# Two gated layers over four batches: how the first layer's transposed normalised x is made for batches two to four

## The chip, the core and the metric

The kernel runs on one core of a Trainium2 chip as one launch. The metric is the time of an execution on the device in microseconds (us). Engines have short names in the profile: PE is TensorE, DVE is VectorE, ACT is ScalarE, POOL is GpSimd, and SP is the engine whose queue issues the DMA transfers here. Each engine takes its instructions in the order of its own queue and waits at an instruction until what that instruction needs is there.

## The reference

The input x has 4 batches of 512 tokens with 256 values each, in float32. Two layers follow each other, and both have the same frame:

```
xn = layernorm(x)                    # over the 256 values of a token
s  = mixer(xn)                       # layer 0: xn + rmsnorm(xn @ M) * w ; layer 1: xn + causal attention
g  = silu(ffn(xn))                   # ffn: (silu(xn W1') * (xn W3')) -> Walsh-Hadamard -> W2'
x  = x + s * g
```

W1 and W3 have 1024 rows. M is a 256x256 matrix that the kernel multiplies out from layer 0's weights, and layer 1's attention normalises its input once more before it.

## The kernel before

Everything is float32. PE multiplies 12-bit parts, so each operand is kept as a pair of tiles (hi, lo) and each product is three passes: hi by hi, hi by lo, lo by hi (`mm3`). A pair is made by `split` (lines 59 to 62): ACT copies the source into hi, rounding it, and DVE subtracts hi from the source into lo. For some of layer 0's weights (`w13l`, quarters 2 and 3) POOL does the subtraction.

The work goes batch by batch: layer 0 for batches 0 to 3, then layer 1 for batches 0 to 3. The main stream of a phase is `ffn`, named f_0 to f_3 in the profile's tiles. It goes through 8 chunks of 128 hidden values. In each chunk come twelve 128x512 products into two PSUM banks (gu, from a ring of three), then silu on ACT, the product of both on DVE (tile h, line 364), a split into hh and hl, and twelve down products of 128x256 (line 332) with the W2 that went through the Walsh-Hadamard transform. The up products need xn transposed, with the 256 values on the partitions: the pair xth, xtl of [128, 2, 512].

Beside a phase's main stream run other tasks, cut into steps by `yield`. `Beside` hands them out evenly over the 16 slots of a phase, from the counts `NORM, MIXER, ATT, ATT1, W2P = 3, 3, 18, 6, 12` (line 570). In layer 0 they are:

- `gate` of the batch before: x += s * silu(down result), on ACT and DVE.
- `mixer(b)`: products with M on PE (tile o), copies and squares on ACT, a pow on POOL (ssr, line 420), four scalings on DVE (osb, line 422) and one addition xn + osb of 128x1024 on POOL (line 425).
- `norm(0, b + 1)`: the next batch's normalisation, which the change is about.
- In phase 0 also the preparation of layer 0's weights (`prep_first`), in phase 1 the preparation of layer 1's W2 (`prep_w2`: butterflies w2b on DVE, lines 125 and 126, a split into w2bh and w2bl, products on PE, splits from PSUM into w2h and w2l), and in phase 2 the first normalisation of layer 1.

The order written in the code is not the order in the queues: the framework's scheduler orders each engine's instructions when the program is built. Tiles come from pools. `t4` has ten slots of 512 KB for raw weights, osb, mrb and others, so a load into such a slot waits until the slot's last reader is done.

Before the change, `norm(0, b)` for b = 1 to 3 takes the moments of each token on DVE, the pow on POOL (`ln_r`), and four DVE operations that make xn token by token. Then for each half k of the 256 values `transpose_half` lets PE transpose four 128x128 tiles into a PSUM bank (tile xt_2tp and its like, line 248), and `split` reads this bank. Batch 0 has its own way, `norm_first`. `norm(1, b)` in layer 1 ends with another chain: the second moments (tile mr) are transposed on PE from [128, 8] to [8, 128] (tile mrp), copied by ACT (rows), written by a DMA to DRAM (there) and read back by a second DMA into all 128 partitions (mrb, 512 KB).

Of the kernel before, what the change touches and what calls it, by code (L numbers as in the profile page):

```python
# [11 lines left out]
F32 = mybir.dt.float32  # L12
# float32 kept to the 12 significant bits that one pass of the tensor engine multiplies
# exactly. A float32 value is the exact sum of two of these (hi + lo), so a float32 product
# is three passes: hi*hi + hi*lo + lo*hi; lo*lo lies below float32's rounding.
F32R = mybir.dt.float32r
# [19 lines left out]
def kernel(ctx: ExitStack, tc: tile.TileContext, a: dict, out: bass.AP):  # L36
# [7 lines left out]
    def t4(name, shape, dt=F32):  # L44
        return act.tile(shape, dt, tag="t4", name=name, bufs=10)
# [13 lines left out]
    def split(src, hi, lo, engine=nc.vector):  # L59
        """hi + lo = src, exactly."""  # L60
        nc.scalar.copy(hi, src)  # L61
        engine.tensor_tensor(lo, src, hi.bitcast(F32), ALU.subtract)

    def mm3(o, terms):
        """o = sum over terms of lhs.T @ rhs, each operand a pair (hi, lo)."""
        seq = [(l[0], r[0]) for l, r in terms]
        for l, r in terms:
            seq += [(l[0], r[1]), (l[1], r[0])]
        for n, (l, r) in enumerate(seq):
            nc.tensor.matmul(o, l, r, start=n == 0, stop=n == len(seq) - 1)  # L70

# [1 line left out]
    xs = {}  # L73

# [3 lines left out]
    def load_x(b, nt=NT):  # L78
        xs[b] = x_slot(f"x{b}", [P, NT, D])
        src = a["x"][b].rearrange("(t p) d -> p t d", p=P)  # L80
        for t in range(0, NT, nt):
            nc.sync.dma_start(xs[b][:, t : t + nt, :], src[:, t : t + nt, :])

    ident, had_f, mask = (wp.tile([P, P], F32, name=n) for n in ("ident", "had_f", "mask"))
# [28 lines left out]
    def prep_w2(layer, raws, dst, scratch):  # L113
        """Rows of W2 under the Walsh-Hadamard transform (it is symmetric, so it may act on
        W2 in place of the hidden values): over the 8 blocks by butterflies, over the 128
        rows of a block by a product with the +-1/32 matrix."""
        w2h, w2l = dst
        for half in range(2):
            ds_ = slice(half * P, (half + 1) * P)
            cur = raws[half]  # L120
            for st, h in enumerate((1, 2, 4)):
# [6 lines left out]
                yield  # L128
            # in float32 it costs TensorE two passes more, but no split beforehand
            native = layer == 0 and half == 0  # L130
# [22 lines left out]
    def product_of_weights(name, lhsT, rhs, nk, scale=None):  # L153
        """[256, 256] = lhsT.T @ rhs over nk chunks of 128, in float32, as a (hi, lo) pair."""
        hi = wp.tile([P, 2, D], F32R, name=f"{name}h")
# [22 lines left out]
    def prep_m(win, wout):  # L178
        """xi*(sum of C_real*B_real - C_imag*B_imag) between W_in and W_out is one matrix."""
        cb = wp.tile([P, 4, 2, DS], F32, name="cb")  # L180
# [29 lines left out]

# [1 line left out]
    def moments(name, x, mr):  # L212
        """mr[:, 0] = the tokens' means, mr[:, 1] = their 1 / sqrt(variance + eps)"""
        st = act.tile([P, NT, 6], F32, tag="stats", name=f"{name}st", bufs=4)
# [9 lines left out]
    def layernorm(name, x, y, groups=(NT,)):  # L224
        """y = layernorm(x), the token tiles in groups of these sizes"""
        t0 = 0
# [36 lines left out]
    def norm_first():  # L263
        """norm(0, 0), each token tile on its own"""
        xn = act.tile([P, NT, D], F32, tag="xn", name="xn0_0", bufs=3)
# [4 lines left out]
        for t in range(NT):  # L270
# [3 lines left out]
            split(o, hi[:, :, sl(t)], lo[:, :, sl(t)])  # L274

    def norm(layer, b):
        xn = act.tile([P, NT, D], F32, tag="xn", name=f"xn{layer}_{b}", bufs=3)
        hi = act.tile([P, 2, S], F32R, tag="xt", name=f"xth{layer}_{b}", bufs=4)
        lo = act.tile([P, 2, S], F32R, tag="xt", name=f"xtl{layer}_{b}", bufs=4)
        xns[layer, b], xTs[layer, b] = xn, (hi, lo)  # L280
        layernorm(f"ln{layer}_{b}", xs[b], xn)
        yield
        if layer:
            # The second normalisation acts on the transposed values: its moments as rows of
            # all tokens, in every partition.
            mr = act.tile([P, 2, NT], F32, tag="mr", name=f"mr{b}", bufs=2)
            moments(f"ln2_{b}", xn, mr)
            yield
            o = psum(f"mrp{b}", [2 * NT, P])
            nc.tensor.transpose(o, mr.rearrange("p a t -> p (a t)"), ident)  # L290
            rows = act.tile([2 * NT, P], F32, tag="rows", name=f"rows{b}", bufs=1)
            nc.scalar.copy(rows, o)
            there = dram.tile([2 * NT, P], F32, tag="rows", name=f"there{b}")
            nc.sync.dma_start(there, rows)
            mrb = t4(f"mrb{b}", [P, 2, S])
            nc.sync.dma_start(
                mrb, there.rearrange("(a t) p -> a (t p)", a=2).unsqueeze(0).to_broadcast([P, 2, S])
            )
            mrs[b] = mrb
            yield  # L300
            return
        for k in range(2):
            o = transpose_half(f"xt{layer}_{b}", xn, k)
            split(o, hi[:, k, :], lo[:, k, :])
            yield

# [3 lines left out]
    def ffn(name, xT, w13, w2, slot, defer=1, spare=(), last=None, parts=1, behind=False):  # L310
        """Up, silu gate, down with the transformed W2: two PSUM banks of two token tiles.
        The down products of a chunk follow the up products of the defer-th after it.
        spare: pairs of tiles that hold the split hidden values of the first chunks.
        last: called with each token tile's result, finished one after the other, each in a
        bank of its own."""
        w2h, w2l = w2
# [7 lines left out]
        def down(c, hh, hl, tiles=range(NT)):  # L324
            for t in tiles:
                o = outs[t]
                for n, (l, r) in enumerate(((hh, w2h), (hh, w2l), (hl, w2h))):
# [7 lines left out]

                    # A start clears the accumulate bits of its whole bank: the bank's second
                    # tile begins without one, behind the first's.
                    if first and t % 2 == 1 and last is None:
# [39 lines left out]
        if last is None:  # L378
            for q in queue:
                down(*q)  # L380
            return dn
        # the later tokens' products stay behind, for the ends of the earlier tokens to run beside
        (q0, q1, q2, q3), ts_ = queue, range(NT)
# [10 lines left out]
    def gate(name, dn, s, x, store=None):  # L394
        """x += s * silu(dn), a pair of token tiles at a time."""
        for i in range(2):
# [8 lines left out]
    def mixer(b):  # L405
        """xn += rmsnorm(xn @ M) * norm_w"""
        xn, xT, m = xns[0, b], xTs[0, b], first["m"]
# [20 lines left out]
    def attention(b):  # L428
        """The transposed xn, split; then xn += causal attention of the normalised, scaled and
        shifted xn"""  # L430
        xn, wqk, wvo = xns[1, b], first["wqk"], first["wvo"]
# [29 lines left out]
        def scores(i0):  # L461
            """Masked scores of two query tiles"""
            if i0:
# [10 lines left out]
        def softmax(i0, scs):  # L474
            """The two exponentials follow each other, for ScalarE changes its table for them."""
            nmax = act.tile([P, 2], F32, tag="nmax", name=f"nmax{b}_{i0}", bufs=4)
# [53 lines left out]
    class Beside:  # L530
        """Steps of other work, spread over the slots of a feed-forward block."""

# [26 lines left out]
    def some(gen, n):  # L559
        """The next n steps of gen"""  # L560
        for _ in range(n):
            next(gen)
            yield
# [4 lines left out]

    # steps of each; an attention's first ones (up to its scores) run a phase ahead of the rest
    NORM, MIXER, ATT, ATT1, W2P = 3, 3, 18, 6, 12  # L570

# [1 line left out]
    load_x(0, 1)  # L573
    # TensorE's clock rises only after a while of work: these products of zeros run while the
    # first loads are under way.
    zeros = hid("zeros")
# [44 lines left out]

# [1 line left out]
    dn = None  # L623
# [35 lines left out]

# [1 line left out]
    def store(b):  # L661
# [38 lines left out]
def _rows(w):  # L700
    """[r*128, n] -> [128, r, n]"""
    return w.reshape(-1, P, w.shape[1]).transpose(1, 0, 2)


def _w13(w1, w3):
    """Columns of W1.T and W3.T in turns of 128, in four parts of [128, 2, 512]."""
    w = np.stack([w1.T.reshape(2, P, NH, P), w3.T.reshape(2, P, NH, P)], axis=3)
    return w.reshape(2, P, 4, S).transpose(2, 1, 0, 3)


def _w2(w2):
    """W2.T as [half of d][128, 8 blocks, 128]."""
    return w2.T.reshape(NH, P, 2, P).transpose(2, 1, 0, 3)
# [45 lines left out]
```

## Time and profile before

| | |
|---|---|
| median of 3 runs | 374.34 us (374.17 to 375.75) |
| profiled execution, first to last instruction | 370.9 us |
| the profiled execution's own whole time | not listed apart; the runs' median lies 3.4 us above its span |
| PE busy | 361.5 us (97%), 2167 instructions |
| DVE busy | 248.0 us (67%), 519 instructions |
| ACT busy | 179.7 us (48%) |
| POOL busy | 36.2 us (10%), 30 instructions |
| one broadcast mrb<-there, 512 KB, from issue to landing | 3.7 us |
| one load x<-in_x, 512 KB, from issue to landing | 3.7 us |

The profile is of one execution. A line of a timeline has the start in us, the duration in us, the engine, the source line, the operation, and "out<-in" by the tiles' names; "x2" means that two instructions are drawn together in it, and the bracket at the end is idle time before it and the instruction that ended it. Matmuls are pipelined and overlap each other in these lines, so PE's pace is read from one start to the next. The slices cut the span in 40 equal parts, a digit being the busy share in tenths. A wait counts only where an engine on the chain of waits has to sit through it.

### The profile page before, as it was taken

The numbers are of one execution on the slowest core, as the hardware profiler recorded it, in microseconds if no ns is written. First come the engines' busy times: TensorE is split into PE (matmuls) and PEld (weight loads), VectorE is DVE, ScalarE is ACT, GpSimd is POOL, SyncE is SP. The second block draws the span as 40 slices with busy tenths as digits, with TensorE's granted clock in tenths as the row PEclk, the third lists the DMA queues.
The fourth block names the chain that finished last, engine by engine and source line by source line (L and its number), as shares of the span: only waits on it lengthen the run. The fifth ranks groups of instructions, "written<-read, shape, count | busy, mean of one in ns | idle before, by whom it ended". The sixth has DMA issues, their size and how long they took to land.

```text
span 370.9 us, 5491 instructions
## 1 busy us (share of the span) xinstructions
PE 361.5 (97%) x2167; PEld 318.2 (86%) x2167; DVE 248.0 (67%) x519; ACT 179.7 (48%) x334; POOL 36.2 (10%) x30
## 2 busy tenths in 40 slices
PE   6997999999999999999999999999999999999995
PEld 4875999888888898889888998988989898888895
DVE  6898948996499339945949487465846447374644
ACT  2765334624453335445553654266633646356451
POOL 2060023410025002400011000010000000000000
PEclk9999999999999999999999999999999999999999
DMA  7915200000000040110010001100003000010001
GB/s 234 389 51 203 80 2 1 2 0 2 0 3 0 0 171 0 58 57 2 1 59 0 0 2 57 59 1 2 0 2 114 2 0 1 2 57 2 1 2 57
DMA packets 8969, 15.50 MB, mean 42 GB/s; under 512 B 848, under 2 KB 6640, under 8 KB 8944
## 3 DMA queue, kind: packets, MB, share of 16 engines
q1 hardware_dynamic: 8944, 15.16, 11.7%
q8 instruction: 17, 0.28, 0.3%
q14 instruction: 8, 0.07, 0.1%
HBM read 13.04 MB, written 2.11 MB: 41 GB/s over the span
## 4 chain that ended last, share of the span: by engine, by line
PE 90%; DVE 5%; DMA 2%; SPq 1%; issue 0%; ACT 0%; DVEq 0%
PE f_3gu L70 12%; PE f_2gu L70 12%; PE f_1gu L70 12%; PE f_0gu L70 8%; PE f_0dn L332 6%; PE f_3dn L332 6%; PE f_1dn L332 6%; PE f_2dn L332 6%; PE sc L70 4%; PE pv L70 4%; PE o L70 3%; PE v L70 3%; PE tq L70 3%; DMA w2raw<-in_w 2%; DVE w2b L125 1%; PE pt L498 1%
## 5 line engine op out<-in xcount | busy, mean ns | idle before, releaser
L70 PE MATMUL f_0gu<-xtl,w13h 128*128 128x512 f32 (+1 forms) x68 | 25.8, 382 | 0.0
L70 PE MATMUL f_1gu<-xth,w13l 128*128 128x512 f32 x64 | 25.5, 399 | 0.0
L70 PE MATMUL f_0gu<-xth,w13l 128*128 128x512 f32 (+1 forms) x68 | 25.5, 384 | 0.0
L70 PE MATMUL f_3gu<-xtl,w13h 128*128 128x512 f32 x64 | 25.5, 398 | 0.0
L70 PE MATMUL f_2gu<-xth,w13l 128*128 128x512 f32 x64 | 25.3, 396 | 0.0
L70 PE MATMUL f_3gu<-xth,w13l 128*128 128x512 f32 x64 | 25.3, 396 | 0.0
L70 PE MATMUL f_1gu<-xtl,w13h 128*128 128x512 f32 x64 | 25.3, 396 | 0.0
L70 PE MATMUL f_2gu<-xtl,w13h 128*128 128x512 f32 x64 | 25.3, 395 | 0.0
L70 PE MATMUL f_0gu<-xth,w13h 128*128 128x512 f32 (+1 forms) x68 | 21.3, 393 | 2.5 <-DVE f_0h L364 2.5
L364 DVE TENSOR_TENSOR f_2h<-f_2h,f_2gu 128x512 f32<-128x512 f32 x16 | 10.9, 681 | 19.1 <-PE f_2gu L70 11.0
L61 ACT CAST f_2hh<-f_2h 128x512 fp32r<-128x512 f32 x16 | 9.9, 621 | 23.0 <-DVE f_2h L364 23.0
L70 PE MATMUL f_2gu<-xth,w13h 128*128 128x512 f32 x64 | 20.7, 397 | 0.0
L70 PE MATMUL f_1gu<-xth,w13h 128*128 128x512 f32 x64 | 20.7, 398 | 0.0
L70 PE MATMUL f_3gu<-xth,w13h 128*128 128x512 f32 x64 | 20.6, 397 | 0.0
L61 ACT CAST f_3hh<-f_3h 128x512 fp32r<-128x512 f32 x16 | 9.9, 620 | 19.7 <-DVE f_3h L364 19.7
L332 PE MATMUL f_3dn<-w2l,f_3hh 128*128 128x256 f32 x64 | 17.6, 281 | 0.0
L332 PE MATMUL f_2dn<-w2l,f_2hh 128*128 128x256 f32 x64 | 17.6, 282 | 0.0
L332 PE MATMUL f_3dn<-w2h,f_3hh 128*128 128x256 f32 x64 | 17.5, 281 | 0.0
L332 PE MATMUL f_2dn<-w2h,f_2hh 128*128 128x256 f32 x64 | 17.5, 281 | 0.0
L332 PE MATMUL f_1dn<-w2l,f_1hh 128*128 128x256 f32 x64 | 17.4, 281 | 0.0
L332 PE MATMUL f_1dn<-w2h,f_1hh 128*128 128x256 f32 x64 | 17.3, 281 | 0.0
L363 ACT ACTIVATE f_2h<-f_2gu 128x512 f32<-128x512 f32 x16 | 9.5, 596 | 16.0 <-PE f_2gu L70 16.0
(227 smaller groups left out, 1104.4 us busy)
## 6 DMA issues: line engine op xcount, KB each, us to landing
w13raw<-in_w SPq DMA_DIRECT2D x8, 512.0 KB, 6.2
w2raw<-in_w SPq DMA_DIRECT2D x4, 512.0 KB, 6.8
mrb<-there SPq DMA_DIRECT2D x4, 512.0 KB, 3.7
x<-in_x SPq DMA_DIRECT2D x3, 512.0 KB, 3.7
out<-x SPq DMA_DIRECT2D x6, 256.0 KB, 2.1
x<-in_x SPq DMA_DIRECT2D x4, 128.0 KB, 2.2
qkraw<-in_qk SPq DMA_DIRECT2D x1, 512.0 KB, 4.7
voraw<-in_vo SPq DMA_DIRECT2D x1, 512.0 KB
```

Source lines behind the costliest of these rows:

```text
L61: nc.scalar.copy(hi, src)
L70: nc.tensor.matmul(o, l, r, start=n == 0, stop=n == len(seq) - 1)
L125: nc.vector.tensor_tensor(nv[:, :, 0], cv[:, :, 0], cv[:, :, 1], ALU.add)
L332: return nc.tensor.matmul(o, l[:, sl(t)], r[:, c, :], start=start, stop=stop, skip_group_check=True)
L363: nc.scalar.activation(h, gu[0], AF.Silu)
L364: gates.append(nc.vector.tensor_tensor(h, h, gu[1], ALU.mult))
L498: nc.tensor.transpose(pt[:, sl(j)], p[:, sl(j)], ident)
```

## The change

For batches 1 to 3 of layer 0, PE no longer transposes the normalised x. The host hands over a transposed copy of the input (`xT`), of which 512 KB a batch are loaded into a tile xTraw. `norm_both` takes the tokens' mean and 1/sqrt(variance + eps) (tile mr), sends them through the chain mrp, rows, there, mrb that layer 1 already had (now a function, `rows_everywhere`), makes xn token by token as before for the mixer and the gate, and then normalises the transposed copy on DVE: for each half, a subtraction of the broadcast means, a multiplication by the broadcast factors, and the split, whose source is now in SBUF. The step count of a normalisation goes from 3 to 4. Layer 1 does the same as before. Comments were dropped, which is left out here.

```diff
     def load_x(b, nt=NT):
...
+        if b:
+            xTraw[b] = t4(f"xTraw{b}", [P, 2, S])
+            nc.sync.dma_start(xTraw[b], a["xT"][b])
...
+    def rows_everywhere(name, mr):
+        o = psum(f"mrp{name}", [2 * NT, P])
+        nc.tensor.transpose(o, mr.rearrange("p a t -> p (a t)"), ident)
+        rows = act.tile([2 * NT, P], F32, tag="rows", name=f"rows{name}", bufs=1)
+        nc.scalar.copy(rows, o)
+        there = dram.tile([2 * NT, P], F32, tag="rows", name=f"there{name}")
+        nc.sync.dma_start(there, rows)
+        mrb = t4(f"mrb{name}", [P, 2, S])
+        nc.sync.dma_start(
+            mrb, there.rearrange("(a t) p -> a (t p)", a=2).unsqueeze(0).to_broadcast([P, 2, S])
+        )
+        return mrb
+
+    def norm_both(b):
...
+        mr = act.tile([P, 2, NT], F32, tag="mr", name=f"mr0_{b}", bufs=2)
+        moments(f"ln0_{b}", x, mr)
+        yield
+        mrb = rows_everywhere(f"0_{b}", mr)
+        for t in range(NT):
+            nc.vector.tensor_scalar(
+                xn[:, t, :], x[:, t, :], mr[:, 0, t : t + 1], mr[:, 1, t : t + 1],
+                ALU.subtract, ALU.mult,
+            )
+        yield
+        for k in range(2):
+            f = xTraw[b][:, k, :]
+            nc.vector.tensor_tensor(f, f, mrb[:, 0, :], ALU.subtract)
+            nc.vector.tensor_tensor(f, f, mrb[:, 1, :], ALU.mult)
+            split(f, hi[:, k, :], lo[:, k, :])
+            yield
+
     def norm(layer, b):
+        if layer == 0:
+            yield from norm_both(b)
+            return
...
-        for k in range(2):
-            o = transpose_half(f"xt{layer}_{b}", xn, k)
-            split(o, hi[:, k, :], lo[:, k, :])
-            yield
...
-    NORM, MIXER, ATT, ATT1, W2P = 3, 3, 18, 6, 12
+    NORM, MIXER, ATT, ATT1, W2P = 4, 3, 18, 6, 12
...
         "x": v["L0_attn_x"],
+        "xT": v["L0_attn_x"].transpose(0, 2, 1).reshape(B, 2, P, S).transpose(0, 2, 1, 3),
```

More of the change, by code (lines that the diff above doesn't have):

```diff
@@ L70, in mm3 @@
             nc.tensor.matmul(o, l, r, start=n == 0, stop=n == len(seq) - 1)
-    xs = {}
+    xs, xTraw = {}, {}
     def x_slot(name, shape):
@@ L274, in norm_first @@
             split(o, hi[:, :, sl(t)], lo[:, :, sl(t)])
+    def rows_everywhere(name, mr):
[11 more added lines that the diff above has]
+    def norm_both(b):
+        xn = act.tile([P, NT, D], F32, tag="xn", name=f"xn0_{b}", bufs=3)
+        hi = act.tile([P, 2, S], F32R, tag="xt", name=f"xth0_{b}", bufs=4)
+        lo = act.tile([P, 2, S], F32R, tag="xt", name=f"xtl0_{b}", bufs=4)
+        xns[0, b], xTs[0, b] = xn, (hi, lo)
+        x = xs[b]
+        mr = act.tile([P, 2, NT], F32, tag="mr", name=f"mr0_{b}", bufs=2)
[14 more added lines that the diff above has]
+            yield
     def norm(layer, b):
+        if layer == 0:
+            yield from norm_both(b)
+            return
         xn = act.tile([P, NT, D], F32, tag="xn", name=f"xn{layer}_{b}", bufs=3)
@@ L282, in norm @@
         yield
-        if layer:
-            mr = act.tile([P, 2, NT], F32, tag="mr", name=f"mr{b}", bufs=2)
-            moments(f"ln2_{b}", xn, mr)
-            yield
[L289 to L301, printed above, removed]
-        for k in range(2):
-            o = transpose_half(f"xt{layer}_{b}", xn, k)
-            split(o, hi[:, k, :], lo[:, k, :])
-            yield
+        mr = act.tile([P, 2, NT], F32, tag="mr", name=f"mr{b}", bufs=2)
+        moments(f"ln2_{b}", xn, mr)
+        yield
+        mrs[b] = rows_everywhere(str(b), mr)
+        yield
     def after(ins):
```

## The prediction

> **What bounds the kernel now.** I read the page's slices and chain first, then the tables by stretch, then the order in time of PE, VectorE (DVE) and GpSimd (POOL) around the lines that the diff touches.
>
> ```profile
> PE   6997999999999999999999999999999999999995
> PEclk9999999999999999999999999999999999999999
> PE 90%; DVE 5%; DMA 2%; SPq 1%; issue 0%; ACT 0%; DVEq 0%
> ```
>
> PE is full in every slice behind the fourth, at a full granted clock, and holds 90% of the chain. From one PE start to the next (0.233 us behind a 128x512 product, 0.118 behind a 128x256 one) no gap is left from 42 us to the end. So PE work taken out there shortens the run one for one, and a wait put in there lengthens it one for one. Other engines count where PE waits for them. The last such wait lies in the start stage, and the chain shows what the removed work is:
>
> ```profile
> 31.43 0.73 PE L70 MATMUL f_0gu<-xth,w13h 128*128 128x512 f32 x2 [2.50 <-DVE f_0h L364]
> ```
> ```profile
> 70.82 0.87 PE xt_2tp L248 x8
> ```
>
> How near DVE is to being the bound, by stretch (columns: length, then busy time of PE, weight loads, DVE, ACT, POOL):
>
> ```profile
> 0.00:36.00 36.00, 30.55 (x133) 23.34 (x134) 30.39 (x56) 18.55 (x31) 8.74 (x11) 1.00 0.62 213
> 58.00:95.00 37.00, 37.00 (x215) 32.32 (x214) 29.99 (x55) 16.13 (x33) 6.11 (x4) 1.00 0.01 1
> 95.00:133.00 38.00, 38.00 (x229) 33.37 (x229) 25.63 (x58) 15.63 (x33) 6.85 (x5) 1.00 0.05 20
> ```
>
> The second row is batch 1's phase: DVE is busy 30 of 37 us there, for it carries the preparation of layer 1's W2 beside the rest. PE doesn't wait, but narrowly: chunk 2's low half f_1hl ends at 79.48 and its down product starts at 79.94 (0.46 us of slack), chunk 3's f_1h ends 80.08 for 80.89 (0.8).
>
> Why DVE is late at times, though its operations are short, stands in the lines of DVE and POOL together:
>
> ```profile
> 20.31 6.31 POOL L62 TENSOR_TENSOR w13l<-w13raw,w13h 128x1024 fp32r<-128x1024 f32 x2 [13.46 <-ACT w13h L61]
> 55.69 2.41 POOL L425 TENSOR_TENSOR xn<-xn,osb 128x1024 f32<-128x1024 f32 x1 [1.85 <-DVE osb L422]
> 73.00 2.41 POOL L425 TENSOR_TENSOR xn<-xn,osb 128x1024 f32<-128x1024 f32 x1 [1.85 <-DVE osb L422]
> ```
> ```profile
> 21.45 0.68 DVE L364 TENSOR_TENSOR f_0h<-f_0h,f_0gu 128x512 f32<-128x512 f32 x1
> 22.04 2.32 DVE L62 TENSOR_TENSOR early<-f_0h,early 128x512 fp32r<-128x512 f32 x1
> 24.29 2.88 DVE L125 TENSOR_TENSOR w2b<-w2b 128x512 f32<-128x512 f32 x1
> ```
> ```profile
> 73.36 3.12 DVE L62 TENSOR_TENSOR w2bl<-w2b,w2bh 128x1024 fp32r<-128x1024 f32 x1
> ```
> ```profile
> 56.00 1.29 DVE L62 TENSOR_TENSOR xtl<-xt_1tp,xth 128x512 fp32r<-128x512 f32 x2 [0.45 <-ACT xth L61]
> ```
>
> A DVE operation with two SBUF inputs (early, w2b, w2bl) takes 2.3 to 3.1 us while a POOL operation runs, against 0.68 or 1.23 alone; one that reads PSUM (f_0gu, xt_1tp) is not delayed. The splits that the change removes are of the second kind, and all that it puts in their place are of the first.
>
> **The change, part by part.** The sum is made on the profiled execution's span, 370.9 us; the median of the runs, 374.34, lies 3.4 above it, for what is around the span, and I add that at the end.
>
> *PE.* Out go 8 transposes a batch, 0.87 us in the row above, 24 in all: -2.6. In comes one transpose of 8 rows a batch (mrp), about 0.11 each: +0.3. Net -0.77 a batch, -2.3 in all, all of it on the bound engine.
>
> *DVE's own work.* Per batch, four 128x512 operations come in (two subtractions, two multiplications) at a step of 0.60 us (17.84 to 18.44 to 19.04 among its rows): +2.4. moments() in place of layernorm() adds a copy of 128x4, below 0.2. The two splits stay, from SBUF now. [...] I take 0.
>
> *The new chain.* Moments, pow on POOL (1.0), mrp on PE, rows on ACT, two DMAs on SP, then DVE. Layer 1 has the same chain: rows at 127.98 for 0.25, its DMA at 128.26, the broadcast issued 1.28 later, landing 3.7 later (page). So 5.2 us from mrp's end to the values in all partitions. Before, PE itself handed x over.
>
> *DMAs.* Six 512 KB transfers more (three xTraw, three mrb) and three small ones, all on SP; ACT and POOL issue none. x1 to x3 and xTraw1 are issued by 37 us. Behind them SP waits in order for rows0_1 (50.5), and w2raw of layer 1, before at 33.8, is issued behind it, at about 53. Landing takes 5.3 to 8.4 by its own rows: 58 to 61, with its first use at 62.85. I take 0; at worst 1 us more of crowding on DVE. xTraw3's slot and the other transfers have tens of us. POOL's order changes too: three pows (1.0 each) stand ahead of the first mixer's; their moments are ready by 47 to 50, so 0.
>
> *Start stage.* The scheduler's order for DVE changes: the next W2 butterflies (w2b<-w2b, two SBUF inputs) now stand ahead of f_0h's multiplication of chunk 2, which before ran at 21.45 untouched by POOL. They get caught under the w13l operations, and f_0h behind them ends near 27.3 in place of 22.1. PE then waits from 24.6 to about 27.4, and 0.65 more for w2bh; the 2.5 to 2.7 us wait at 31.43 falls away in exchange. Net +0.75, bounds -0.5 (the butterflies get in before POOL) and +2 (both waits stay in part).
>
> *Batch 0 to 1.* PE would reach f_1's first product at 57.9 (58.0 less 0.78 of transposes, plus 0.75 of lag). mrp0_1 stands behind the mixer's products, at about 49; rows 50.3, its DMA 50.6, broadcast 51.9, landed 55.6. But POOL's addition xn0+osb runs from about 54.9 to 57.3, and the subtraction has two SBUF inputs. So: start 57.25, subtraction, multiplication and half the second pair to 59.05, ACT's cast (0.55) to 59.6, PE at 59.7. Wait: +1.8. Without the lock 0.5; with the DMAs at their upper durations 2.5. [...]
>
> *Batch 1.* The same four operations for batch 2 (2.4 us) enter the stretch in which DVE has 7 us free of 37 and PE's slack is 0.46 to 0.8, with DVE 1.7 behind at its start. In my walk of DVE's new order with the old durations chunk 2's f_1h ends at 77.9, w2bl (again under POOL's addition) at 81, and f_1hl at 84. PE waits 0.8, 1.2, 1.1 and 0.2 for these: +3.3, bounds +1 (order kinder, DVE catches up in its idle spots) and +4.5.
>
> *Batch 2.* DVE waits in its queue for mrb0_3 (about 1.9 us; mrp0_3 sits late in the phase), and f_2's hidden values queue behind it. Their slack here is 1.0 at the least and mostly over 2: 0, bounds 0 and +1. Later phases have slacks of 2 us and more and unchanged work: 0.
>
> Sum: -2.3 + 0.75 + 1.8 + 3.3 = +3.55, span 374.5, time 377.9. As a wait in the start stage lets DVE catch up a little for the next, I shade it to 377.5.
>
> **Rivals.** A, as above, chance 0.55: 375.9 to 380.5. B, chance 0.21: the same mechanism, but one of the two large waits is absorbed (by the slack at the boundary, xth's 2.05 us in the trace of before, or by DVE's 7 idle us): +0.3 to +1.7, so 374.6 to 376.0. C, the other side, chance 0.14: DVE never gets behind PE. Its place is the w2bl under POOL's addition at 73; if the shifted phases take these two apart, each of the waits of batch 1 (3.3) and the port's part of the boundary (1.3) falls off and what is left is PE's 2.3 against 0.75 and 0.5: about -1.0, and with no wait at all -2.3 (-2.8 with the start's lower bound): 371.5 to 373.3, the lower half likelier, for what spares batch 1 spares the boundary too. It decides where the new DVE work delays chunk 2's and 3's values by less than their 0.46 to 0.8 us. Against it: 2.4 us of new work in front of a 0.46 us slack. D, chance 0.10: the delays feed back through the ring of three PSUM banks of the up products, PE's waits delay DVE's inputs and so on: +7 (5 to 9), so 381. That the change doesn't take the transposes off PE is excluded by the code: xt of layer 0 is gone for batches 1 to 3.
>
> **How the numbers follow.** The likeliest case gives 377.5. About 0.5% (1.9 us, so 372.5 to 376.2) is what a measurement of this kernel can tell from no change. A lies above it for nearly all of its width (0.53 of 0.55), D wholly (0.09 counted); B lies within, with the rest of A and D; C counts 0.12 below and 0.02 within. Faster 0.12, same 0.26, slower 0.62. The range leaves out D's upper half and C's tail: 372.0 to 381.5.
>
> **What would show it.** Right: between 57 and 60 us a PE wait of 1 to 2.5 us, on ACT's xth with DVE's subtraction at 2 us or more beside POOL's addition; PE waits of some 3 us in 75 to 90, on f_1h and f_1hl, with a w2bl of 3 us near; a PE wait at about 25 in place of the one at 31; busy PE about 2.3 less; no PE wait in batch 2. Wrong: no PE gap behind 45 us (then about 372), or a gap for w2raw, xTraw or mrb3, which I priced at nothing.

## The result, and the profile after

The changed kernel takes 376.23 us (median of 14 runs, 375.21 to 377.82), the kernel before 373.78 in the same comparison (median of 14). The ratio is 1.007, with a 95% interval of 1.0051 to 1.0089: slower by 1.9 to 3.3 us. The profiled execution after has a span of 375.8 us and took 377.55 as a whole, 1.3 above its median; what lies around a span is thus 1.75 us. Single executions lie up to 3.7 us apart before and 2.6 after, so below waits are compared by the traces and times by medians and ratios.

The page of the changed kernel, in the same lines as shown of before:

```profile
PE   7979998989999999999999999999999999999995
PEclk9998999999999999999999999999999999999999
PE 87%; DVE 6%; DMA 2%; POOL 2%; ACT 1%; issue 1%; SPq 0%; DVEq 0%; POOLq 0%
```

A slice is 9.4 us here. PE's row has an 8 at 56 and at 75 us, where before it was full, and the chain holds a POOL share of 2%. From 85 us on the row is as before. The 8 in the clock's row, at 28 us, is told of in the last section. In the table by stretch (length, then busy time of PE, weight loads, DVE, ACT, POOL, then granted clock), batch 1's phase stands out:

```profile
36.00:58.00 22.00, 22.00 (x149) 20.39 (x148) 15.48 (x54) 8.87 (x23) 5.82 (x5) 1.00 0.22 62
58.00:95.00 37.00, 33.64 (x192) 28.57 (x192) 34.81 (x61) 16.62 (x35) 6.79 (x3) 1.00 0.17 61
95.00:133.00 38.00, 38.00 (x224) 33.15 (x223) 23.95 (x57) 15.85 (x34) 5.91 (x4) 1.00 0.10 32
```

DVE went from 30.0 to 34.8 busy us of 37, PE lost 3.4. Batch 2's phase, behind it, has no PE wait. The timeline of PE names every wait, in the brackets:

```profile
26.78 0.73 PE L70 MATMUL f_0gu<-xth,w13h 128*128 128x512 f32 x2 [2.20 <-DVE f_0h L391]
...
61.05 0.74 PE L70 MATMUL f_1gu<-xth,w13h 128*128 128x512 f32 x2 [1.04 <-ACT xth L61]
...
79.38 0.73 PE L70 MATMUL f_1gu<-xth,w13h 128*128 128x512 f32 x2 [0.61 <-DVE f_1h L391]
...
82.34 0.74 PE L146 MATMUL w2ps<-w2bl,had 128*128 128x512 f32 x2 [0.82 <-DVE w2bl L62]
...
85.35 0.39 PE L359 MATMUL f_1dn<-w2h,f_1hl 128*128 128x256 f32 x1 [0.88 <-DVE f_1hl L62]
```

Measured from one start to the next, less the step of the product in front, these waits are 2.4 (start stage), 1.20 (into batch 1), and 0.78, 0.99 and 1.04 in batch 1; one of 0.15 follows at 90.5. I use this measure from here on. Behind 42 us they add up to 4.16. Less the 2.3 us of PE work saved, that is +1.85; with +0.6 from the start stage (first experiment) the sum is +2.45, the measured difference of the medians. That they agree to the last digit is luck, for the interval of the ratio is 1.4 us wide.

Why DVE was late in batch 1 is in the timelines of POOL and of DVE, first after the change, then before it:

```profile
56.19 2.40 POOL L452 TENSOR_TENSOR xn<-xn,osb 128x1024 f32<-128x1024 f32 x1 [1.79 <-DVE osb L449]
73.22 3.80 POOL L447 TENSOR_TENSOR ssr<-ssr,mhalf 128x4 f32<-128x4 f32 x1 [14.63 <-DVE ssr L446]
78.80 2.40 POOL L452 TENSOR_TENSOR xn<-xn,osb 128x1024 f32<-128x1024 f32 x1 [1.79 <-DVE osb L449]
```
```profile
57.90 1.84 DVE L312 TENSOR_TENSOR xTraw<-xTraw,mrb 128x512 f32<-128x512 f32 x2 [1.79 <-DMA mrb<-there]
...
77.05 1.67 DVE L449 SCALAR_TENSOR_TENSOR osb<-osb,ssr,nwb 128x256 f32<-128x256 f32 x4 [0.91 <-POOL ssr L447]
78.64 0.68 DVE L391 TENSOR_TENSOR f_1h<-f_1h,f_1gu 128x512 f32<-128x512 f32 x1
79.24 3.05 DVE L62 TENSOR_TENSOR w2bl<-w2b,w2bh 128x1024 fp32r<-128x1024 f32 x1
```
```profile
68.56 2.59 POOL L420 TENSOR_TENSOR ssr<-ssr,mhalf 128x4 f32<-128x4 f32 x1 [3.27 <-DVE ssr L419]
```
```profile
71.18 1.67 DVE L422 SCALAR_TENSOR_TENSOR osb<-osb,ssr,nwb 128x256 f32<-128x256 f32 x4 [0.90 <-POOL ssr L420]
72.77 0.68 DVE L364 TENSOR_TENSOR f_1h<-f_1h,f_1gu 128x512 f32<-128x512 f32 x1
```

The pow on four values a partition takes 1.01 us in most places and 3.80 here in the changed kernel: between 73.05 and 76.14 DVE runs two-input operations back to back (w2b, the new multiplications on xTraw, f_1hl), each at 0.68 to 0.69, and this time POOL's operation is the one drawn out. DVE then waits 0.91 at osb for the pow, f_1h stands behind osb in its queue, and PE waits 0.78 for f_1h. POOL's addition falls on w2bl, which takes 3.05 in place of about 1.23, and PE waits 0.99 for w2bl and 1.04 for f_1hl, which stands behind it. Where the prediction and the expectations speak of a lock or of a shared port, these lengths are what is measured; what in the chip draws the operations out, no run shows.

Neither collision is new. Before the change the pow took 2.59, DVE waited 0.90 for it at osb, and w2bl took 3.12 under the addition (the prediction shows that line). PE had slack for it: f_1h of chunk 2 ended at 73.44, 2.5 us before the product that needs its bank started at 75.97. After the change this f_1h ends at 79.32, 5.9 us later, while PE's queue gets there only 2.6 later. Of the 3.3 between them, 2.4 are the four new operations; the rest DVE brings along from its late entry into the phase (its first operation of the gate starts 4.0 later than before, PE's first product 3.0).

### The profile page after: what moved, and what is told of

The parts are those of the page before. It is cut to its first block, busy times and chain, and to the rows that moved or that the text cites. A ratio compares the mean times of both kernels' runs of the same rounds, so it can differ in the third digit from the quotient of the medians.

```text
span 375.8 us, 5490 instructions
## 1 busy us (share of the span) xinstructions
PE 363.9 (97%) x2146; PEld 318.3 (85%) x2146; DVE 254.1 (68%) x534; ACT 180.5 (48%) x337; POOL 36.4 (10%) x30
## 4 chain that ended last, share of the span: by engine, by line
PE 87%; DVE 6%; DMA 2%; POOL 2%; ACT 1%; issue 1%; SPq 0%; DVEq 0%; POOLq 0%
PE f_3gu L70 12%; PE f_2gu L70 12%; PE f_0gu L70 10%; PE f_1gu L70 10%; PE f_3dn L359 6%; PE f_2dn L359 6%; PE f_1dn L359 5%; PE sc L70 4%; PE pv L70 4%; PE f_0dn L359 4%; PE o L70 3%; PE v L70 3%; PE tq L70 3%; DVE w2b L128 1%; DVE w2b L129 1%; DMA mrb<-there 1%
## 5 line engine op out<-in xcount | busy, mean ns | idle before, releaser
L70 PE MATMUL f_0gu<-xth,w13h 128*128 128x512 f32 (+1 forms) x68 | 22.2, 406 | 2.2 <-DVE f_0h L391 2.2
L61 ACT CAST f_1hh<-f_1h 128x512 fp32r<-128x512 f32 x16 | 9.9, 620 | 15.7 <-DVE f_1h L391 15.7
```

## The experiments

Each ran against the kernel before. "Over" is the ratio less one, times that kernel's median of 373.3 to 373.5 us.

**1. The start stage by itself.** The diff changes one number that looks like bookkeeping: a normalisation counts as 4 steps, and `Beside` hands out steps by that count. Here the kernel before has the new count in phase 0 and nothing else.

```diff
-            tasks.append((norm(0, b + 1), NORM))
+            tasks.append((norm(0, b + 1), NORM if b else 4))
```

> The kernel before with one number changed: the step count of the normalisation in phase 0 is given as 4 instead of 3 (the steps themselves stay 3). It moves the W2 butterflies of the start ahead of f_0h as in the changed kernel; nothing else of the change is in it. Theory (the start stage's order costs by itself): the PE wait near 31 us goes, one near 24 to 27 comes, +0.3 to +1.0 us over before. Rival (the two waits swap for nothing, the whole loss lies behind 57 us): within 0.2 us of before.

Measured: 375.02 against 373.46, ratio 1.0029 (1.0005 to 1.0053). DVE's order in the start is that of the changed kernel, and the wait moved from 28.5 to 24.2 with a second one behind it:

```profile
27.04 0.73 PE L70 MATMUL f_0gu<-xth,w13h 128*128 128x512 f32 x2 [2.43 <-DVE f_0h L364]
...
30.58 0.74 PE L142 MATMUL w2ps<-w2bh,had 128*128 128x512 f32 x2 [0.48 <-ACT w2bh L61]
```

Summed from start to start, less the median step of each form of product, PE loses 10.96 us in this trace and 10.35 in before: +0.6. The ratio says +1.1. The difference is in line with the clock that is listed with each run: runs with a mean of 0.993 to 0.995 take about 2 us longer in this comparison than those near 1.0 (last section), and 8 of the 12 runs here are such, but 10 of before's 29. Run against run at the higher clock the medians differ by 0.5 (373.15 and 372.65), at the lower one by 0.6 (375.19 and 374.61). So the start stage's cost is real, and it comes from a step count, not from the new operations.

**2. The changed kernel with that count put back** to 3 in phase 0.

> The changed kernel with the step count of the normalisation in phase 0 put back to 3, so that the start stage has the order of before. Theory: the changed kernel's time less what the start stage costs, 0.3 to 1.0 us, so +1.4 to +2.1 us over before, with the waits at 60 us and in 78 to 91 us as they were. Rival (start order free): +2.4 us as the changed kernel.

Measured: 378.35, ratio 1.0132 (1.01 to 1.0164), +4.9 us; a clear miss. The wait into batch 1 is 3.23 us here, not 1.20:

```profile
60.40 0.82 PE L70 MATMUL f_1gu<-xth,w13h 128*128 128x512 f32 x2 [3.07 <-ACT xth L61]
```

The count had also moved mrp0_1 in PE's queue. Call the PE work that is queued between mrp0_1 and f_1's first product the cover. Counted in the queue and priced at 0.233 and 0.118 us a product, it is 8.85 us in the changed kernel and 6.84 here. The chain from mrp to xth is equally long in both: mrp at 50.8 and the product at 61.05, and 50.2 and 60.40. So the wait is about 10.1 less the cover: 1.2 and 3.2. Behind the long wait PE's 128x512 products lie 0.43 us apart until 64.2 instead of 0.233 (granted clock 0.95 over 58 to 95 us), which took about 1.6 more. The listed clock of all six runs is 0.990 to 0.995.

**3. Only batches 2 and 3 the new way.** Batch 1 keeps PE's transposes (`if layer == 0 and b in (2, 3)`), and the start stage is that of before.

> Only batches 2 and 3 are normalised the new way, batch 1 by PE as before: no change of the start stage and no late hand-off between batch 0 and 1, but the four additional VectorE operations for batch 2 lie in batch 1's phase. Theory (crowding of VectorE in batch 1's phase under POOL's lock makes the waits by itself): 1.5 us of PE work saved, waits of 1.5 to 3 us there, so 0 to +1.5 us over before. Rival (those waits come only because VectorE enters the phase late): no waits, -1.5 us.

Measured: 375.66, ratio 1.0056 (1.0033 to 1.0078), +2.1 us. The waits in batch 1's phase are 1.12, 0.75, 0.92, 0.43 and 0.24, together 3.5, more than I gave them. Less 1.5 of PE work that is +1.9. DVE enters the phase on time here, so the late entry isn't needed for these waits. The collision is another one: the pow takes 1.02 and w2bl 1.21, but POOL's addition (3.92 in place of 2.40) meets a pair of the new multiplications, which takes 2.89 in place of 1.29:

```profile
76.73 3.92 POOL L457 TENSOR_TENSOR xn<-xn,osb 128x1024 f32<-128x1024 f32 x1 [4.46 <-DVE osb L454]
```
```profile
78.91 2.89 DVE L313 TENSOR_TENSOR xTraw<-xTraw,mrb 128x512 f32<-128x512 f32 x2
```

**4. No POOL addition in batch 1's mixer.**

```diff
-        nc.gpsimd.tensor_tensor(xn, xn, osb, ALU.add)
+        if b != 1:
+            nc.gpsimd.tensor_tensor(xn, xn, osb, ALU.add)
```

> The changed kernel without POOL's addition xn+osb of batch 1 (so batch 1's s lacks the mixer's product; the output differs for that batch). Theory (the shared port makes w2bl late): w2bl takes 1.2 instead of 3.05 us, and the PE waits at 81 and 84 us (1.0 each) go while the first of 0.8 at 78.5 stays: 2 us below the changed kernel, +0.4 us over before. Rival (VectorE has simply too much to do there): w2bl shorter, but the waits stay within 0.4 us, +2.0 to +2.4 us over before.

Measured: 374.46, ratio 1.003 (1.001 to 1.0051), +1.1 us where I expected +0.4, and 1.8 us below the changed kernel's median. In its DVE timeline w2bl is back to its own length:

```profile
78.31 1.22 DVE L62 TENSOR_TENSOR w2bl<-w2b,w2bh 128x1024 fp32r<-128x1024 f32 x1
```

Of the three waits the first stays (0.77), the second is gone, and the third is 0.31. The pow still takes 3.80.

**5. Neither POOL instruction in batch 1's mixer:** the pow of ssr is left out too (`if b != 1:` ahead of it). DVE's work is the changed kernel's.

> The changed kernel without POOL's two instructions in batch 1's mixer: neither the pow of ssr nor the addition xn+osb (batch 1's s is wrong for it). VectorE's work is as in the changed kernel. Theory (the waits of batch 1 are the shared port's: the first because POOL's pow is locked out for 3.8 us by VectorE's back-to-back operations and osb and f_1h stand behind it in VectorE's queue, the second and third because the addition locks out w2bl): all three waits go, none over 0.3 us is left in 62 to 95 us, 2.5 to 3 us below the changed kernel, -0.5 to 0 us against before. Rival (too much VectorE work for the phase): waits of 0.8 us or more stay.

Measured: 373.37 against 373.39, ratio 1.0 (0.9977 to 1.0023). Two waits of 0.12 and 0.16 are left in batch 1's phase, and w2bl and f_1h are on time, with DVE as full as in the changed kernel:

```profile
58.00:95.00 37.00, 36.00 (x206) 30.95 (x207) 33.43 (x63) 18.72 (x38) 0.00 (x0) 1.00 0.11 36
```

(The 1.0 us that PE misses here is the wait into batch 1, unchanged at 1.20, whose greater part lies behind 58.) DVE's fullness alone makes PE wait for almost nothing. That the first wait is due to the pow being drawn out to 3.80, and not to there being a pow, wasn't run apart; but an undisturbed pow (1.01 from 73.22) would be done before DVE comes to osb at 76.14.

**6. Without the four new operations for batch 2:** its transposed x goes unnormalised into the split, and POOL's two instructions stay.

```diff
-            nc.vector.tensor_tensor(f, f, mrb[:, 0, :], ALU.subtract)
-            nc.vector.tensor_tensor(f, f, mrb[:, 1, :], ALU.mult)
+            if b != 2:
+                nc.vector.tensor_tensor(f, f, mrb[:, 0, :], ALU.subtract)
+                nc.vector.tensor_tensor(f, f, mrb[:, 1, :], ALU.mult)
```

> The changed kernel without the subtractions and multiplications of batch 2 (its transposed x is used as loaded, so batch 2's result is wrong): 2.4 us of two-input VectorE work less in batch 1's phase, with POOL's pow and addition kept and w2bl still behind osb and f_1h in VectorE's queue. Theory (the new operations are what pushes POOL's two and VectorE's later ones together): the waits of 3.0 us in 78 to 91 us shrink to 0 to 0.8, so 2.2 to 3 us below the changed kernel. Rival (the port's collisions come by the order alone, whoever fills VectorE): 1.5 us or more of them stay.

Measured: 373.96, ratio 1.0011 (0.9988 to 1.0034), 2.3 below the changed kernel; no wait in batch 1's phase. w2bl is still caught under POOL's addition, while the pow takes 1.01:

```profile
76.65 2.83 DVE L62 TENSOR_TENSOR w2bl<-w2b,w2bh 128x1024 fp32r<-128x1024 f32 x1
```

So it takes both. The collisions with POOL cost DVE 0.9 and 1.8 us, which PE's slack covered before; 2.4 us of new operations use that slack up. The ratio shows less than the trace, by which this version would be 0.5 below before (-2.3 + 0.6 + 1.2): 10 of its 12 runs are at the lower clock, and 7 of before's 35.

**7. Only batch 1 the new way.**

> Only batch 1 is normalised the new way. Theory (parts add up): start stage +0.6, boundary wait +1.2 or a little more as PE comes to it earlier, 0.8 saved, no wait in batch 1's phase beyond: +1.0 to +1.5 us over before. Rival (batch 1's waits come from the late entry into the phase, not from batch 2's new operations): the 3 us of waits come as well, +3.5 to +4.5 us.

Measured: 374.38, ratio 1.0034 (1.0014 to 1.0055), +1.3 us. There is a wait of 1.03 into batch 1 (cover counted as above 9.09, so the chain is 10.1 again) and none in its phase. The parts add up: 0.6 + 1.0 - 0.8 = +0.8, within the interval (0.5 to 2.1).

**8. Only batch 3 the new way.**

> Only batch 3 is normalised the new way. Theory (batch 2's phase has slack enough for the late broadcast and the additional VectorE work): PE does 0.77 us less and waits for nothing new, -0.8 us against before. Rival (the late mrb0_3 or f_2's hidden values cost something there): 0 or above.

Measured: 373.09 against 373.26, ratio 0.999 (0.9976 to 1.0005). PE has no new wait behind 42 us. The 0.8 us saving lies within the interval, but the runs don't tell it from nothing.

**9. The normalisation ahead of the mixer in phase 0.** If the wait into batch 1 is chain less cover, the chain has to start earlier in PE's queue.

```diff
+        if b == 0:
+            tasks.append((norm(0, 1), NORM))
         tasks.append((mixer(b), MIXER))
-        if b + 1 < B:
-            if b:
-                load_x(b + 1)
+        if b and b + 1 < B:
+            load_x(b + 1)
             tasks.append((norm(0, b + 1), NORM))
```

> The changed kernel with batch 1's normalisation ahead of batch 0's mixer in the list of tasks of phase 0, so that mrp0_1 has 12.2 us of PE work (by the steps 0.233 and 0.118) between itself and f_1's first product instead of 8.9. Theory (the wait at the boundary is the length of the chain mrp to xth, 10.2 us, less that cover): the wait of 1.2 us goes, 1.2 us below the changed kernel, +1.0 to +1.4 us over before, with the waits in 78 to 91 us kept. Rival (the port and VectorE's queue set it): the wait stays at 0.8 us or more.

Measured: 372.54 against 373.26, ratio 0.9971 (0.9954 to 0.9989): faster than before. The wait into batch 1 is gone, ACT's xth being complete at 55.9 for PE at 58.2, as forecast; but the waits within batch 1 are gone too, which I had not forecast. In the timelines of POOL and DVE both collisions are gone:

```profile
67.62 1.02 POOL L447 TENSOR_TENSOR ssr<-ssr,mhalf 128x4 f32<-128x4 f32 x1 [6.62 <-DVE ssr L446]
70.43 2.79 POOL L452 TENSOR_TENSOR xn<-xn,osb 128x1024 f32<-128x1024 f32 x1 [1.78 <-DVE osb L449]
```
```profile
82.71 1.22 DVE L62 TENSOR_TENSOR w2bl<-w2b,w2bh 128x1024 fp32r<-128x1024 f32 x1
```
```profile
58.00:95.00 37.00, 37.00 (x214) 32.23 (x213) 33.11 (x61) 17.26 (x35) 6.20 (x3) 1.00 0.08 30
```

The second fence is DVE's line of w2bl, the third the row of batch 1's phase. The mixer's part of DVE's and POOL's work comes earlier in the phase, so the pow meets no run of two-input operations (1.02), and w2bl comes 9 us after the addition instead of under it. Whether that or the earlier place of the mixer's work counts for more was not tested. DVE is as full as ever (33.1 of 37), and PE is full.

**10. As 9, with the step count of phase 0 at 3.**

```diff
-            tasks.append((norm(0, 1), NORM))
+            tasks.append((norm(0, 1), 3))
```

> The changed kernel with the normalisation ahead of the mixer in phase 0 and the step count of phase 0 at 3 (the start stage in the order of before); layer 1's W2 stays in phase 1. Theory (both repairs add): the start stage's 0.6 us comes off the version with the normalisation ahead, no wait behind 45 us, -1.3 to -2.0 us against before, 0.4 to 0.9 us below the version with the normalisation ahead alone. Rival (the other order brings the port's collisions in batch 1 back): waits of 1 us or more in 62 to 95 us, at or above before's time.

Measured: 372.05 against 373.39, ratio 0.9962 (0.9942 to 0.9981), -1.4 us, the fastest version. No PE wait lies behind 42 us. Two short ones at 37 and 38 us (0.6 and 0.24) are new, waits for w2h and for f_0h in the start stage, and keep it from the full 2.3. It is not told from version 9 by these intervals.

```profile
PE 361.1 (98%) x2146; PEld 316.5 (86%) x2146; DVE 252.4 (68%) x534; ACT 180.8 (49%) x337; POOL 37.1 (10%) x30
```

**11. As 10, and layer 1's W2 prepared in phases 1 and 2** (5 and 7 of its 12 steps, `some(w2_steps, 5)` in phase 1 and the rest in phase 2), to empty batch 1's phase.

> The changed kernel with three orders altered: the normalisation ahead of the mixer in phase 0, the step count of phase 0 at 3 as in before, and the preparation of layer 1's W2 spread over phases 1 and 2 (5 and 7 of its 12 steps) instead of all in phase 1. Theory (each PE wait of the changed kernel comes from where the work was put, not from the new work itself): no new PE wait, only the saving of 2.3 us on PE, -1.5 to -2.3 us against before. Rival (VectorE's four operations a batch are too many wherever they lie): waits come up in phase 2, -0.5 to +1.5 us.

Measured: 372.08, ratio 0.9974 (0.9952 to 0.9997), about -1.0 us. It is faster than before, but the rival's waits do come up in phase 2: 0.49 at 115 us and 0.52 at 121. It gains nothing over version 10, which needs no split.

**12. The same split in the kernel before,** as a control.

> Control: the kernel before with the preparation of layer 1's W2 spread over phases 1 and 2 in the same way. PE waits for nothing there in before, so both theories expect no difference, within 0.3 us.

Measured: 373.45, ratio 1.0013 (0.9999 to 1.0027). The time agrees with no difference, my premise doesn't: PE waits 0.22 and 0.75 us at 117 to 118 us, for w2bh and for f_2's hl. Phase 2 had less room than its 25.6 busy us of 38 suggested.

## Why the prediction was right, and where it was off

The result lies in the forecast range, on the forecast side, by the mechanism of case A, at the lower end of A's 375.9 to 380.5. The signs of all terms were right, and their sum was too high. By its terms:

- *PE's saving, -2.3.* Shown by the count (2167 to 2146 instructions: 24 out, 3 in) and by experiments 9 and 10, where nearly only it is left: with the small waits of their start stages it adds up to -1.2 and -1.5, and the ratios give -1.1 and -1.4. The sign that I named for it, "busy PE about 2.3 less", was a bad one: busy PE rose from 361.5 to 363.9, since a matmul's record was longer at half rate (0.63 us for a 128x512 product at 28.16 us, 0.39 at 27.35), and in front of a wait a product counts with its whole record (0.40 at 24.19) instead of its step (0.233). Starts and counts tell PE's work, its busy sum doesn't.
- *Start stage, +0.75.* 0.6 by the trace of experiment 1. Its cause is the step count.
- *Batch 0 to 1, +1.8.* 1.20. I made POOL's addition the deciding share, 1.3 of it (1.8 less the 0.5 without it). In the trace mrb landed at 57.9, 0.7 before the addition ended, and the two subtractions took 1.84 where a pair takes 1.29; the addition's part is about 0.55. The chain itself I had too short: from mrp's end to mrb's landing it took 6.8 us and not 5.2, for ACT took rows up only at 51.93, and the broadcast needed 4.4. The length of the chain against PE's cover set the wait, and three covers (9.09, 8.85, 6.84) gave it to 0.1 us. A greater cover (12.1, experiment 9) removed it; the chain is shorter there, too (9.1), since mrb lands (52.4) before POOL's addition starts (58.6), and the two subtractions take 1.29.
- *Batch 1, +3.3.* 2.96 in four waits, near 78.5, 81.2, 84.1 and 90.5, for the tiles that were named and for the reason that was named: new DVE work in front of a small slack, with w2bl under POOL's addition as before. What the account leaves out is the pow, behind which DVE's queue stands for 0.91 us, as it did before the change. For batch 1 the prediction counted only DVE's operations as drawn out (w2bl, which took 3.05), and here POOL's pow was, too (3.80). Experiments 4 and 5 split the 2.96: the addition 1.7, the pow most of the rest. Experiment 6 shows that without the new operations PE waits for neither.
- *Batch 2 and what I priced at nothing.* No wait there, none for w2raw, xTraw or mrb3: right. The splits' new source cost and gained nothing either: the six subtractions of xtl with xTraw as source, in SBUF, took 0.684 us (median) in the changed kernel, those with PSUM as source 0.677 to 0.686 before.
- *The sum's base.* I took 3.4 us for what lies around a span, from a profiled execution against the median of other runs; it is 1.75. The profiled execution of before was one of the quicker ones: the median of 373.78 stands for a span of 372.0 and not 370.9. So the errors cancel in part: the base span was 1.1 too low, the increase 1.1 too high (3.55 for 2.45), what lies around it 1.65 too high, and 0.4 was taken off; the point forecast of 377.5 is 1.3 too high. That the predicted span of 374.5 is the median's (376.23 - 1.75) is luck.
- *The rivals.* B's absorption didn't happen. C named its deciding point as w2bl under POOL's addition, and that was right in part: taken apart by experiment 4 alone, they leave 1.2 of the 2.96. Experiments 9 and 10 are case C, reached by another order of the same work, and there the pow takes 1.02, too. D, a runaway through the ring of banks, didn't show.

## What to carry to other kernels

Work that goes off a full engine pays only if what takes its place arrives before that engine asks for it: write down the new chain's length and count the cover in the bound engine's queue, for their difference is the wait (10.1 less 8.85 us here). Where VectorE operations with two SBUF inputs are added, look for every GpSimd instruction near them, in both directions, a tiny one included: here a pow on four values a partition took 3.80 us instead of 1.01, and w2bl 3.05 instead of 1.23. Such a collision may cost nothing as long as the bound engine has slack behind it; new work on the same queue is what makes it cost. An interleaver's step counts and task order are part of a change: with both put right, the same arithmetic went from 2.45 us slower to 1.4 us faster than before.

## What the runs showed of the hardware

Behind PE's wait of 2.2 us at 24.6, the changed kernel's PE ran at half rate for one spell; behind before's longer wait of 2.5 us at 28.9 it did not. The rows by stretch show both (the column behind POOL's is the granted clock), first of the changed kernel, then of before:

```profile
24.50:27.91 3.41, 1.21 (x6) 0.95 (x6) 3.41 (x6) 1.15 (x3) 0.48 (x1) 1.00 0.00 0
27.91:31.32 3.41, 3.41 (x10) 2.31 (x9) 3.41 (x7) 1.37 (x3) 0.00 (x0) 0.50 0.52 154
```
```profile
26.74:30.15 3.41, 2.19 (x10) 1.42 (x8) 3.41 (x7) 0.02 (x1) 0.00 (x0) 1.00 0.29 79
30.15:33.57 3.42, 2.14 (x9) 1.78 (x10) 3.42 (x8) 2.59 (x4) 0.00 (x0) 1.00 0.65 226
```

A 128x512 product steps by 0.427 us in the spell instead of 0.233, about 1.5 us lost. The same wait led to such a spell in the profiles of the changed kernel and of experiments 6 and 7 (granted clock down to 0.50 in rows between 27 and 32 us), and to none in those of experiments 1, 5 and 9 (1.00 in the same rows).

In the clock's records of these two traces the stretches of one rate are whole multiples of 3.41 us long, and they lie differently in each execution: in the changed kernel's full rate from 10.85 to 27.91 (5 times), half rate to 31.32 (once), full rate to 376.07 (101 times); in before's full rate from 6.27 to 371.49 (107 times). In the changed kernel's the 3.41 us in front of the spell, which hold most of the wait, leave PE 1.21 busy us. In before's, cells of that length counted from 6.27 have a boundary at 30.15, which cuts the wait in two, and the cells leave PE 2.19 and 2.14. In experiment 7's profile PE is 0.79 us busy between 24 and 27, and from 27 to 30.4 the granted clock is 0.51. That a cell with little PE work brings the half rate on is my reading of these few cases; no run tested it, and where a limit would lie is not shown.

The first PE products run at half rate in both traces: the seven warm products of 128x512 take 0.628 us each (median), as in the spell. The eight wqkps products, which start at 8.0 us, take 0.379 (median) in before's, behind 6.27, and 0.631 in the changed kernel's, in front of 10.85.

For the reader of profiles it means that the wait of 2.2 us cost 3.7 here, and that the 1.5 of half rate in it come in some executions of a kernel and not in others: of the 14 runs of the changed kernel five have a listed clock of 0.995, as the profiled one with its one spell, and a median of 377.55 us, and nine have 1.0 and a median of 376.01. How often it happens differed between the kernels: below 0.996 are 20 of the 99 runs of before listed with the experiments, and 49 of 86 runs of the changed kernel and of experiments 1, 4 to 7 and 9, whose start stage has the new order.
